# A list-scheduled attention and expert kernel: the routing chain of a chunk gets an earlier key, and row transfers by index a shorter spacing near the end

## Chip, core and metric

The kernel runs on one core of a Trainium2 chip. The metric is the device time of one execution in microseconds (us); lower is better. All arithmetic is float32.

## What is computed

The input is 16 sequences of 256 tokens with 128 channels. Four layers follow each other, each added to its input after a layer norm:

```python
x = x + attn_a(layernorm(x))   # 8 heads of 16, causal, a rank-1 term added to the scores
x = x + ffn(layernorm(x))      # 8 experts, top 2 by a router, hidden width 512
x = x + attn_b(layernorm(x))   # 16 heads of 8, no mask
x = x + ffn(layernorm(x))      # the same expert layer and weights again
```

In `ffn` each token goes to the two experts with the largest router logits; their outputs are added with softmax weights, and the sum with the token goes through one more layer norm with gamma and beta.

## The kernel before

**Layers and chunks.** The layers are called a (first attention), B (first expert layer), b (second attention) and D (second expert layer). A "batch" is one sequence of 256 tokens. The expert layers work on chunks of batches: B in chunks of 2, 4, 5 and 5 batches, D in chunks of 4, 4, 3, 2, 2 and 1. They are called B0 to B3 and D0 to D5.

**One chunk of an expert layer** (`experts`). Router logits come batch by batch (L768, kept at L777). When the last batch's logits are there, a chain of some 29 short VectorE instructions (L930 to L1100), with two groups of matmuls inside (L1005 `dt`, L1015 to L1023 `dr`), finds for each token the two rows in a list sorted by expert. Its results are `idx` (L1077, the rows), `dti` (L1100, which expert each tile of 128 rows belongs to) and, a little later, `rw` (L981, the weights). GpSimd then scatters the tokens to these rows of a DRAM buffer, 128 tokens a transfer (L1113, `xs`). SyncE loads the rows back four tiles at a time (L1158), TensorE turns them (L1169, `xt`), and for each tile multiplies by the first weight matrix (L1182, `h`), ScalarE and VectorE apply the bias and relu (L252 and L1189, `hT`), TensorE multiplies by the second (L1206, `o`), VectorE takes the result out of PSUM (L1214), and SyncE stores it (L1219, `os`). The weights of a tile's expert (578 KB) are loaded anew for each tile (L1150). GpSimd gathers the two rows of each token back, 128 tokens a transfer (L1271, `r0` and `r1`), VectorE sums them (L1296, `y`), and the last layer norm follows (L302, L304, L309 and L310 on GpSimd, L796, L804). The last chunk D5 has one batch and goes through all eight experts without sorting (L848, L861, L869, L877, L881).

**Order of the work.** Nothing is issued in the order of the source. The kernel first makes a list of tasks, each with an engine, a planned duration, what it needs, the buffers it takes, and a key. A planner at the end of the kernel walks through a clock of its own: on each engine it looks at the tasks that could start within a small slack of the earliest, and takes the one with the smallest key. Keys are counted in pairs of heads: an attention pair of heads has the key of its slot, one more for each pair; a chunk's routing chain has the key `key8`, which is the end of its last batch plus 0.2. What the planner yields is a fixed order for each engine. On the chip each engine runs its list strictly in order: an instruction that waits holds up all behind it.

**Transfers by index.** The planner also spaces these transfers: two of them start at least `GAP` = 2.6 us apart on its clock, and where ScalarE has an instruction that ends in between, the transfer is made to wait for that instruction on the chip too (`apart`), so that the spacing holds there:

```python
if t.eng == "POOL" and t.kb:
    s = max(s, moved[0] + GAP)
...
since = [i for done, i in marks if moved[0] + 1.3 <= done <= s - 0.1]
paced[0] = since[-1] if since else None
```

`all_st` holds the 192 tasks of the second kind of score matmul (L564, `st`, one for each pair of heads of both attentions), and `begun[1]` counts how many of them the planner has placed.

Of the kernel before, what the change touches and what calls it, by code (L numbers as in the profile page):

```python
# [42 lines left out]


LAT = dict(mem=3.0, qk=6.0, sh=2.4, sc=4.0, rows=4.0, we=4.5, os=5.5, g=5.0)

EARLY = 2.0

# [23 lines left out]
def block_kernel(  # L72
# [170 lines left out]
    GAP = 2.6  # L243
# [15 lines left out]
    def apart(i):  # L259
        if paced[0] is not None:  # L260
            tc.add_manual_dep(i.ins, paced[0].name, SYNC, reason="rows by index one by one")
        return i
# [99 lines left out]
    all_s, all_st = [], []  # L362

    def attention(kind, b, slot):
# [80 lines left out]
        if not (causal and b < WIDE):  # L445
# [3 lines left out]
            t_sp = Task("SP", 0.39, spread, ahead - 5, [t_sg], take=[mem_h], use=[qks_h],  # L449
                        kb=256, lat=LAT["mem"])  # L450
            if not causal and "a" in [region_of.get((i, h)) for h in halves]:
                clear = Task("DVE", 0.7, lambda: clear_k(i), ahead - 5, last + [clear])
            t_qk = [Task("SP", 1.5, spread2, ahead - 4, [t_sp, clear] + last, take=[m_h],
                         use=[mem_h], kb=256, lat=LAT["qk"])]

# [88 lines left out]
        t_ms = Task("ACT", 0.26, shift_copy, slot + pairs, [t_mt], use=[mm])  # L544
        t_sh = Task("SP", 0.56 * nq, shift2, slot + pairs, [t_ms], use=[ms_h], lat=LAT["sh"])

# [177 lines left out]
    order = {"last": None, "xs": {}, "os": {}, "n": 0}  # L724

    def experts(layer, c, ends, need, dense=False):
# [13 lines left out]
        rl_h, tgt_h, t_tgt, t_lg, tT_of = Hold("rl"), {}, {}, [], {}  # L740

        for b in bs:
            key = ends[b] + 0.2
            t0 = (b - b0) * NT

            def tgt_tile(b=b):
                g["tgt", b] = work.tile(
                    [P, NT, C], F32, tag="tgt", name=f"tgt_{n}_{b}", bufs=RINGS["tgt"]
                )
                return g["tgt", b]  # L750
            t_tgt[b], tgt_h[b] = normed(
                lambda b=b: xb[b], f"{n}_{b}", key, [at_x[b]], "tgt", tgt_tile)

            def bias(b=b):

                nc.gpsimd.tensor_tensor(
                    xb[b], xb[b], beta_sb.unsqueeze(1).to_broadcast([P, NT, C]), ALU.add
                )
            at_x[b] = Task("POOL", 0.73, bias, key + 3, [t_tgt[b]])
            t_tT, tT, tT_h = turned(  # L760
                lambda b=b: g["tgt", b], f"{n}_{b}", key, [t_tgt[b]], [tgt_h[b]])
            tT_of[b] = tT, t_tT, tT_h
            mm = Hold("mm")

            def logits(b=b, tT=tT):
                g["lg", b] = ps = ps_mm.tile([P, NT, E], F32, tag="mm", name=f"lg_{n}_{b}")
                for t in range(NT):
                    nc.tensor.matmul(  # L768
                        ps[:, t, :], lhsT=tT()[:, t * P:(t + 1) * P], rhs=wr_sb,
                        start=True, stop=True,  # L770
                    )

            def keep_logits(b=b, t0=t0):
                if b == b0:
                    g["rl"] = small.tile([P, ct, E], F32, tag="rl", name=f"rl_{n}",
                                         bufs=RINGS["rl"])
                nc.vector.tensor_tensor(  # L777
                    g["rl"][:, t0:t0 + NT, :], g["lg", b],
                    br_sb.unsqueeze(1).to_broadcast([P, NT, E]), ALU.add,
                )  # L780
            e = Task("PE", 0.26, logits, key, [t_tT], take=[mm], use=[tT_h])
            t_lg.append(Task("DVE", 0.1, keep_logits, key, [e] + t_lg[-1:], use=[mm],
                             take=[rl_h] if b == b0 else []))
# [34 lines left out]
        def every_expert(b, kk, t_gate, rw_h):  # L818
# [16 lines left out]
            def load(e):  # L835
                g["w", e] = work.tile([P, W_N], F32, tag="we", name=f"we_{n}_{e}",
                                      bufs=RINGS["we"])
                nc.sync.dma_start(out=g["w", e], in_=we[e])
# [47 lines left out]
            for e in range(E):  # L886
                w_h, hT_h, z_h, mm3 = Hold("we"), Hold("pT"), Hold("z"), Hold("mm")
                k = kk + 0.5 * e
                e_load = Task("SP", 0.5, lambda e=e: load(e), k - 8, take=[w_h],
                              kb=592, lat=LAT["we"], order=[e_load])  # L890
                t_r = []
# [12 lines left out]


        key = max(ends[b] for b in bs) + 0.2
        key8 = key
        k8 = ct * E
        per = 0.14 + 0.0011 * k8
        shape = [P, ct, E]  # L910
# [119 lines left out]
        e = Task("PE", 0.3, count, key8, chain, take=[mm1])  # L1030
        chain = [e]
        dve(0.27, total, use=[mm1])
        e = Task("PE", 0.6, ranks, key8, chain, take=[mm2])
# [77 lines left out]
        def scatter(t, k):  # L1111
            b = b0 + t // NT
            i = apart(nc.gpsimd.indirect_dma_start(  # L1113
                out=x_rows[0:ne * P, :], out_offset=bass.IndirectOffsetOnAxis(
                    ap=g["idx"][:, k, t:t + 1], axis=0),
                in_=g["tgt", b][:, t % NT, :], in_offset=None,
                bounds_check=ne * P - 1, oob_is_err=False,
            ))

            gr = f"sc_{n}"  # L1120
            tc.declare_no_dep(i.ins, group=gr, reason="each row is written once")
            tc.add_to_no_dep_group(gr, i.ins)
        t_sc = []
        free = order["xs"].get(q, []) + zeroed[q]
        for k in range(2):
            for t in range(ct):
                b = b0 + t // NT
                t_sc.append(Task(
                    "POOL", 1.25, lambda t=t, k=k: scatter(t, k), key + 0.3 + 0.01 * len(t_sc),
                    [t_idx[k]] + free, use=[idx_h, tgt_h[b]], kb=64, lat=LAT["sc"] - 1.3,  # L1130
                ))

# [92 lines left out]
        for i in range(ne):  # L1225
            b, j = divmod(i, TB)
            kk = tile_key(i)
            w_h, hT_h, mm1, mm2 = Hold("we"), Hold("hT"), Hold("mm"), Hold("mm")
            if j == 0:
                x4_h, xT_h, mm3, o4_h = Hold("x4"), Hold("xT"), Hold("mm"), Hold("o4")  # L1230
                e = Task("SP", 0.4, lambda b=b: rows(b), kk - 2.5, t_sc, take=[x4_h],
                         kb=256, lat=LAT["rows"])
                t_rows.append(e)
                e = Task("PE", 0.46, lambda b=b: turn_rows(b), kk - 1, [e],
                         take=[mm3, xT_h], use=[x4_h])
                t_xT = Task("ACT", 0.48, lambda b=b: keep_rows(b), kk - 1, [e], use=[mm3])
                t_out = []
            t_load = Task("SP", 0.95 if j == 0 else 0.5, lambda i=i: load(i), kk - 3,
                          [t_ti], take=[w_h], use=[ti_h], kb=592, lat=LAT["we"], order=[t_load])
            t_up_last = t_up = Task("PE", 0.98, lambda i=i: up(i), kk, [t_load, t_xT],  # L1240
                                    take=[mm1, hT_h], use=[w_h, xT_h], order=[t_up_last],
                                    kind="up")
            t_up.rate = RATES[layer][min(c, len(RATES[layer]) - 1)]
            r1 = Task("DVE", 0.27, lambda i=i: relu_v(i), kk, [t_up], use=[mm1, w_h])
            r2 = Task("ACT", 0.76, lambda i=i: relu_s(i), kk, [t_up], use=[mm1, w_h])
            t_dn = Task("PE", 0.98, lambda i=i: down(i), kk, [r1, r2],
                        take=[mm2, o4_h] if j == 0 else [mm2], use=[hT_h, w_h],
                        order=t_dns[-1:])
            t_dns.append(t_dn)
            t_out.append(Task("DVE", 0.2, lambda i=i: keep_out(i), kk, [t_dn], use=[mm2, w_h]))  # L1250
            loads.append(t_load)
            if j == TB - 1 or i == ne - 1:
                stores.append((i, Task(
                    "SP", 0.4, lambda b=b: store(b), kk, t_out + order["os"].get(q, []),
                    use=[o4_h], kb=256, lat=LAT["os"], lag=LAG_OS)))
# [22 lines left out]
        for b in bs:  # L1278
# [3 lines left out]
            for k in range(2):  # L1282
                r_h = Hold(f"r{k}")
                e = [None]
# [52 lines left out]
    ends = {"B": {}, "D": {}}  # L1337
# [16 lines left out]
    begun = [0.0, 0]  # L1354
    moved = [-GAP]
# [11 lines left out]
    def start(t):  # L1367
        s = max(t.ready + t.lag, free[t.eng])
        if t.eng == "POOL" and t.kb:
            s = max(s, moved[0] + GAP)  # L1370
        if t.kind == "up" and len(all_st) > begun[1]:
            s = max(s, begun[0] + t.rate)
        for h in t.take:
            q, n = rings[h.ring], RINGS[h.ring]
            if len(q) >= n:
                if q[-n].left:
                    return None
                s = max(s, q[-n].done)
            if h.ring == "att" and len(q) > 1:
                if q[-1].left or q[-2].left:  # L1380
                    return None
                s = max(s, q[-1].done, q[-2].done)
        return s
# [34 lines left out]
    while left:  # L1418
        best = None
        for e in ENGS:  # L1420
# [4 lines left out]
            s, t = min(((s, t) for s, t in c if s <= s0), key=lambda st: st[1].key - stay(st[1]))  # L1425
# [3 lines left out]
        s, t, c = best  # L1429
# [94 lines left out]
```

## Time and profile before

| | |
|---|---|
| median of three runs | 945.51 us (942.85 to 948.49) |
| the profiled execution: time, span | 950.31 us, 948.6 us |
| TensorE busy | 889.4 us, 94% of the span |
| VectorE, ScalarE, GpSimd busy | 618.1, 512.6 and 416.9 us |
| indexed transfers, GpSimd time for one | 248, about 1.0 us |
| bytes moved by DMA | 181.96 MB, mean 192 GB/s |
| mean granted TensorE clock | 0.978 |

The profiled execution took 1.7 us more than its span from the first to the last instruction, and 4.8 us more than the median. Every matmul of the source appears twice in the trace. In the rows of the profile PE is TensorE, DVE VectorE, ACT ScalarE, POOL GpSimd and SP SyncE; a name behind "<-" in brackets says what ended a wait.

### The profile page before, as it was taken

The numbers are of one execution on the slowest core, as the hardware profiler recorded it, in microseconds if no ns is written. First come the engines' busy times: TensorE is split into PE (matmuls) and PEld (weight loads), VectorE is DVE, ScalarE is ACT, GpSimd is POOL, SyncE is SP. The second block draws the span as 40 slices with busy tenths as digits, with TensorE's granted clock in tenths as the row PEclk, the third lists the DMA queues.
The fourth block names the chain that finished last, engine by engine and source line by source line (L and its number), as shares of the span: only waits on it lengthen the run. The fifth ranks groups of instructions, "written<-read, shape, count | busy, mean of one in ns | idle before, by whom it ended". The sixth has DMA issues, their size and how long they took to land. (4 is left out here: it accounts for less than half of the span.)

```text
span 948.6 us, 24346 instructions
## 1 busy us (share of the span) xinstructions
PE 889.4 (94%) x8941; PEld 720.4 (76%) x8941; DVE 618.1 (65%) x1919; ACT 512.6 (54%) x1188; POOL 416.9 (44%) x553
## 2 busy tenths in 40 slices
PE   7788899998999999999999999999989999899995
PEld 5555688887887778787777777777767877799985
DVE  4578687778657757456686457745766665564666
ACT  5355565665555664565655555556645655545421
POOL 4134635654653554313554225443534314444633
PEclk9799899999999999999999999999999999999998
DMA  4222667666765587575776767566856675599991
GB/s 128 57 70 73 232 194 208 202 208 194 232 187 186 165 207 183 187 204 176 186 197 192 221 180 202 168 190 208 188 142 192 216 185 166 170 306 348 372 316 36
DMA packets 115191, 181.96 MB, mean 192 GB/s; under 512 B 11904, under 2 KB 79360, under 8 KB 115072
## 3 DMA queue, kind: packets, MB, share of 16 engines
q1 hardware_dynamic: 106704, 163.69, 58.4%
q0 software_dynamic: 7936, 16.27, 5.5%
q8 instruction: 71, 1.16, 0.5%
q10 hardware_dynamic: 432, 0.45, 0.2%
q14 instruction: 48, 0.39, 0.1%
HBM read 145.63 MB, written 34.34 MB: 190 GB/s over the span
## 5 line engine op out<-in xcount | busy, mean ns | idle before, releaser
L510 DVE TENSOR_REDUCE m_b<-s_b 128x4 f32<-128x1024 f32 x128 | 155.8, 1220 | 59.9 <-PE s_b L487 39.5
L252 ACT ACTIVATE pT_b<-st_b 128x1024 f32<-128x1024 f32 x128 | 129.9, 1026 | 68.4 <-PE st_b L564 49.2
L252 ACT ACTIVATE hT_D<-h_D,we_D 128x128 f32<-128x128 f32 (+1 forms) x301 | 89.7, 372 | 103.2 <-issue 34.5
L487 PE MATMUL s_b<-qk 31*128 31x256 f32 x1024 | 134.9, 405 | 4.7 <-DVE m_b L510 3.1
L564 PE MATMUL st_b<-qk 32*128 32x256 f32 x1024 | 131.4, 409 | 3.7 <-issue 1.7
L252 ACT ACTIVATE hT_B<-h_B,we_B 128x128 f32<-128x128 f32 x276 | 81.1, 365 | 75.0 <-DVE hT_B L1189 38.6
L1206 PEld LDWEIGHTS o_D<-we_D,hT_D 128*128 128x128 f32 x760 | 93.6, 192 | 23.6 <-ACT hT_D L252 12.0
L1206 PE MATMUL o_D<-we_D,hT_D 128*128 128x128 f32 x760 | 107.1, 287 | 4.5 <-ACT hT_D L252 2.6
L1206 PE MATMUL o_B<-we_B,hT_B 128*128 128x128 f32 x736 | 106.3, 288 | 3.4 <-ACT hT_B L252 2.8
L1206 PEld LDWEIGHTS o_B<-we_B,hT_B 128*128 128x128 f32 x736 | 90.7, 192 | 24.4 <-ACT hT_B L252 14.2
L1182 PE MATMUL h_D<-xT_D,we_D 128*128 128x128 f32 x760 | 102.4, 282 | 0.1
L1271 POOL DMA_INDIRECT r_B<-os,idx_B x64 | 67.9, 1062 | 75.7 <-DMA we_B<-in_we_dram 21.0
L1182 PE MATMUL h_B<-xT_B,we_B 128*128 128x128 f32 x736 | 100.6, 280 | 0.2 <-ACT xT_B L252 0.2
L1182 PEld LDWEIGHTS h_D<-xT_D,we_D 128*128 128x128 f32 x760 | 92.5, 193 | 9.9 <-issue 7.4
L1113 POOL DMA_INDIRECT xs<-tgt_D,idx_D x60 | 60.1, 1001 | 87.7 <-DVE idx_D L1077 17.9
L1182 PEld LDWEIGHTS h_B<-xT_B,we_B 128*128 128x128 f32 x736 | 89.7, 192 | 10.3 <-issue 8.6
L487 PEld LDWEIGHTS s_b<-qk 31*128 31x128 f32 x1024 | 80.8, 186 | 17.7 <-issue 5.5
L564 PEld LDWEIGHTS st_b<-qk 32*128 32x128 f32 x1024 | 79.1, 188 | 17.2 <-issue 7.2
L1271 POOL DMA_INDIRECT r_D<-os,idx_D x60 | 62.8, 1047 | 62.0 <-ACT hT_D L252 30.4
L1113 POOL DMA_INDIRECT xs<-tgt_B,idx_B x64 | 64.7, 1011 | 50.7 <-ACT hT_B L252 12.8
L500 DVE TENSOR_TENSOR s_a<-s_a,cmask 128x512 f32<-128x512 f32 x64 | 44.6, 697 | 42.7 <-PE s_a L487 22.5
L1189 DVE TENSOR_SCALAR hT_D<-h_D,we_D 128x128 f32<-128x128 f32 x95 | 33.0, 350 | 56.7 <-PE h_D L1182 23.7
(401 smaller groups left out, 1620.0 us busy)
## 6 DMA issues: line engine op xcount, KB each, us to landing
we_D<-in_we_dram SPq DMA_DIRECT2D x103, 578.0 KB
we_B<-in_we_dram SPq DMA_DIRECT2D x92, 578.0 KB
qk<-qkm SPq DMA_DIRECT2D x104, 64.0 KB
x_B<-xs SPq DMA_DIRECT2D x20, 256.0 KB
os<-o_B SPq DMA_DIRECT2D x20, 256.0 KB
x_D<-xs SPq DMA_DIRECT2D x20, 256.0 KB
os<-o_D SPq DMA_DIRECT2D x20, 256.0 KB
qkm<-qks_b SPq DMA_DIRECT2D x16, 256.0 KB
```

Source lines behind the costliest of these rows:

```text
L252: i = getattr(nc.scalar, name)(*args, **kw)
L487: nc.tensor.matmul(ps[:, j, col:col + nk], lhsT=qT[r:r + 31, t * P:(t + 1) * P], rhs=kT[r:r + 31, 0:nk], start=True, stop=True,)
L500: nc.vector.tensor_tensor(dg, dg, cmask.unsqueeze(1).unsqueeze(1).to_broadcast([P, 2, 2, P]), ALU.add,)
L510: nc.vector.tensor_reduce(m[:, :, heads].rearrange("p t j -> p j t"), ps.rearrange("p j (t k) -> p j t k", k=T), axis=AX.X, op=ALU.max, ne ...
L564: nc.tensor.matmul(ps[:, j, col:col + T - q0], lhsT=kT[r:r + 32, t * P:(t + 1) * P], rhs=qT[r:r + 32, q0:T], start=True, stop=True,)
L1113: i = apart(nc.gpsimd.indirect_dma_start(out=x_rows[0:ne * P, :], out_offset=bass.IndirectOffsetOnAxis(ap=g["idx"][:, k, t:t + 1], axis=0) ...
L1182: nc.tensor.matmul(ps[:, f, :], lhsT=w[:, f * P:(f + 1) * P], rhs=g["xT", b][:, j * P:(j + 1) * P], start=True, stop=True,)
L1189: nc.vector.tensor_scalar(g["hT", i][:, f, :], g["h", i][:, f, :], g["w", i][:, W_B1 + f:W_B1 + f + 1], 0.0, ALU.add, ALU.max)
L1206: nc.tensor.matmul(ps, lhsT=g["hT", i][:, f, :], rhs=g["w", i][:, W_2 + f * C:W_2 + (f + 1) * C], start=(f == 0), stop=(f == NF - 1),)
L1271: apart(nc.gpsimd.indirect_dma_start(out=g["r", k, b][:, t, :], out_offset=None, in_=o_rows[0:ne * P, :], in_offset=bass.IndirectOffsetOnAxis(
```

## The change

It has three live parts (the first and the third number of `AHEAD` are zero and alter nothing):

```diff
+AHEAD = 0, 6, 0
...
-        key8 = key
+        key8 = key - AHEAD[1]
...
                 e = Task("PE", 0.46, lambda b=b: turn_rows(b), kk - 1, [e],
-                         take=[mm3, xT_h], use=[x4_h])
+                         take=[mm3, xT_h], use=[x4_h], order=[order.get("turn")])
+                order["turn"] = e
...
         if t.eng == "POOL" and t.kb:
-            s = max(s, moved[0] + GAP)
+            s = max(s, moved[0] + (GAP if len(all_st) > begun[1] + 24 else 1.4))
```

- The tasks of the routing chain up to `dti` get a key that is smaller by six pairs of heads. The four tasks of the weights `rw` keep theirs (`gates` sets `key8` anew).
- The turns of rows (`turn_rows`, L1169) are placed in the order of the chunks and blocks; before, a later block could be turned first.
- Once at most 24 of the 192 `st` tasks are left to place, the spacing of transfers by index drops from 2.6 to 1.4 on the planner's clock.

No instruction is added or taken away on any engine. The order changes on all of them.

More of the change, by code (lines that the diff above doesn't have):

```diff
@@ L742, in experts @@
         for b in bs:
-            key = ends[b] + 0.2
+            key = ends[b] + 0.2 - AHEAD[0]
             t0 = (b - b0) * NT
@@ L1128, in experts @@
                 t_sc.append(Task(
-                    "POOL", 1.25, lambda t=t, k=k: scatter(t, k), key + 0.3 + 0.01 * len(t_sc),
+                    "POOL", 1.25, lambda t=t, k=k: scatter(t, k), key + 0.3 - AHEAD[2] + 0.01 * len(t_sc),
                     [t_idx[k]] + free, use=[idx_h, tgt_h[b]], kb=64, lat=LAT["sc"] - 1.3,
```

## The prediction

> **What bounds the kernel now.** I read the page first (engines, then the slices), then windows, then the waits of each engine, then timelines around the stalls.
>
> ```profile
> span 948.6 us, 24346 instructions
> PE 889.4 (94%) x8941; PEld 720.4 (76%) x8941; DVE 618.1 (65%) x1919; ACT 512.6 (54%) x1188; POOL 416.9 (44%) x553
> PE   7788899998999999999999999999989999899995
> DMA  4222667666765587575776767566856675599991
> ```
>
> PE is at work for 94% of the span, and no other engine comes near. The whole prize is 948.6 - 889.4 = 59 us of idle PE. The windows say where it lies:
>
> ```profile
> 0.00:25.00 25.00, 17.89 (x106) 14.02 (x106) 12.35 (x48) 14.65 (x33) 10.48 (x29) 1.00 0.44 121
> 650.00:700.00 50.00, 46.52 (x488) 36.29 (x488) 32.45 (x98) 29.82 (x62) 21.52 (x29) 0.97 0.73 188
> 875.00:900.00 25.00, 24.90 (x211) 24.03 (x210) 15.25 (x61) 13.07 (x44) 15.26 (x18) 1.00 1.02 373
> 925.00:949.00 24.00, 13.97 (x96) 12.98 (x94) 15.73 (x55) 3.35 (x8) 9.10 (x12) 0.89 0.12 34
> ```
>
> The columns are PE, PEld, DVE, ACT, POOL, clock, DMA. The first four windows (0 to 100) leave 20.5 us of PE idle. There the PE list of the changed program is the same as before (its first difference is at PE instruction 637 of 4774, about 100 us in). 100 to 600 leaves 15 us, 600 to 825 leaves 12, the rest 12, of which 10 are the last drain. From 850 on the DMA engines are full (1.02) and PE is too.
>
> What a stall looks like, in the timeline of DVE at 689 and of POOL before it:
>
> ```profile
> 683.59 1.12 POOL L1271 DMA_INDIRECT r_D<-os,idx_D  x1 [0.19 <-ACT hT_D L252]
> ...
> 691.63 0.35 DVE L1296 SCALAR_TENSOR_TENSOR y_D<-r_D,rw_D,tgt_D 128x128 f32<-128x128 f32 x1 [2.26 <-DMA r_D<-os,idx_D]
> 692.01 1.22 DVE L510 TENSOR_REDUCE m_b<-s_b 128x4 f32<-128x1024 f32 x1
> ```
>
> DVE reached a sum `y` whose gathered rows had not landed, and stood 2.26 us; behind it in its list was the maximum `m_b`, for which PE waited 2.52 us. The same at the end, milder:
>
> ```profile
> 900.66 6.34 DMA r_D<-os,idx_D
> 907.09 0.35 DVE y_D L1296
> 907.44 0.21 DVE o_D L1214
> 907.65 0.14 issue
> 907.79 1.29 PE o_D L1206 x8
> ```
>
> This is the chain of waits: gather, `y`, the eviction `o_D` behind it, PE, which lost 1.0 us.
>
> Whether the routing chain is late anywhere: for D4, the tightest of the later chunks, the timelines show its last `idx`, the last scatter, the load of its first rows, the turn of these rows.
>
> ```profile
> 843.67 0.16 DVE L1077 CAST idx_D<-dsf_D 128x4 int32<-128x4 f32 x1
> 859.94 0.99 POOL L1113 DMA_INDIRECT xs<-tgt_D,idx_D  x1 [1.24 <-ACT xT_D L252]
> 865.46 0.38 SPq L1158 DMA_DIRECT2D x_D<-xs  x1
> 873.07 0.60 PE L1169 MATMUL xt_D<-ident,x_D 128*128 128x128 f32 x4
> ```
>
> 29 us pass between the places and their first use. For D0 it is 70 (471.44 to 541.13). PE works on other tiles meanwhile. No stall of PE in the trace ends on a row load. So the chain is on no path.
>
> **Part 1, the earlier key.** Nothing is added, so what counts is the order of the two built programs. The chain cannot begin before the last logits, and each step needs the one before, so a smaller key only wins ties against `m_b`, `hT` and evictions. In DVE's list the last `idx` moves by a place or two up to B2 and comes later in D: place 1233 to 1249 for D1, 1674 to 1691 for D4. So "sooner" is hardly delivered, and with 29 us of cover it is worth 0. It may cost: one step is 0.16 to 0.28 us, 29 of them for each of nine chunks, all in front of something PE needs would be some 50 us; none would be 0. To choose I compared the two PE lists. Each full 128-column pass costs 0.112 us (L869, x32 in 3.57 us in the chain). For each task that needs ACT or DVE work on an earlier PE result I took the PE work in between, and counted what it lacks to the lag at which such tasks stall in the trace (1.4 us for `o` after `h`, 0.85 to 2.2 for others). The lacks sum to 71 us before and 73 after; 1.4 of the difference is one place at the very end, costed below. Attention pairs stand two by two in both, and PE changes between its kinds of work 458 times before, 454 after. So part 1 is costed at 0, with 5 either way: that much lies between stretches of the two lists (150 to 200: 4.6 against 2.3; 300 to 350: 2.3 against 4.4). Its cover is PE work of other tiles; without it D4 would show first.
>
> **Part 2, turns in order.** Before, `xt` of D3's first block stands ahead of D2's last; now behind it. 0.33 us of PE work changes places with 0.44. 0.
>
> **Part 3, the closer spacing.** It begins with the pairs of batch 13 (743 us) and touches 60 transfers: D3's and D4's scatters, D1's to D4's gathers. Of these 39 waited for an ACT instruction before, 10 now. Such waits hold the rows of D up by
>
> ```profile
> POOL r_D L1271 <- ACT hT_D L252: 30.4, 19, 3.5
> ```
>
> (total, times, longest). Freed, POOL issues every 1.30 us (0.99 of work, 0.30 of issue). What this buys, place by place:
>
> - D4's scatters: 17.6 us from first to last before, 9.1 now. But the places come later: `dr` of D4 moves from 717.5 to 721.1 us of PE work, its first turn from 751.1 to 750.0, so cover falls from 33.6 to 28.9. Needed: 5 (ranks to `idx`) + 9.1 + 5.5 (last scatter to row load, 859.94 to 865.46) + at most 7.6 (load to turn) = 27.2. It fits, with 1.7 to spare: 0.
> - D3's gathers: 891.8 to 909.6 before; now eight in 10 us. The stall at 907 goes: -1.0.
> - The end. Before, batch 14 ends last since its gathers are issued until 938.66; x15 is done at 942.48, x14 at 945.39. Now the sums of batches 13 and 14 come earlier and x15 ends last: of the 2.9 between the two about 2.1 goes, since 0.6 to 0.8 of batch 14's work still stands ahead of x15. But the PE list now ends o5, o6, h7, o7 where it ended h6, h7, o6, o7. o7 needs `hT` of expert 7, and DVE has before that four `y` (1.2), z and two sums (1.05), statistics (0.75), and `hT` itself (0.88) behind o6's end at about 935.5 and the rest of z5: o7 starts at 938.9 in place of 937.2, +1.7. With DVE's tail behind it the last instruction comes at about 945.5 against 945.39: 0.
> - POOL's queue: batch 14's and 15's norm steps and `bias` stand among gathers in both lists. In SP's list 163 of 811 instructions stand elsewhere among the rest, and the weights' loads keep their order among themselves. The chip shows SP waiting for free buffers most of the time, which PE sets: 0.
>
> Sum: -1.0. The profiled execution goes from 950.3 to 949.3; it was 4.8 above the median, so I put the median at 945.5 - 1.0 = 944.5.
>
> **Two rules against rows.** The gather at 683.59 held DVE until 691.63, 8.0 us; the one in the chain took 6.34. The Trainium skill (DMA: Bandwidth & Descriptors, Anatomy of one DMA) has 2.0 us + bytes / 436e3 for a GpSimd transfer, 2.15 for 64 KB (an estimate by that page). By the rule no gather is ever late here, neither stall exists and closer spacing gains nothing: 945.5. By the rows it can remove stalls of 1.0 and 2.5, or add them. I go by the rows.
> PE's clock in the window around the first stall:
>
> ```profile
> 686.00:698.00 12.00, 9.48 (x99) 6.94 (x94) 7.40 (x26) 4.29 (x9) 3.59 (x4) 0.86 0.68 151
> ```
>
> 0.86 over 12 us is 3.4 us at half clock, 1.7 lost, after 2.5 us of idling. TensorE: Matmul & The Clock Gate (Part 1) lets the clock fall after an idle window of about 3.4 us. By the page a stall of 2.5 costs 2.5, by the row 4.2. I price a long stall at 4.2; two are then 8.4, not 5.0.
>
> **Rivals.** *Slower: sums stand too early in DVE's list.* The planner now believes the rows come 1.4 apart and puts D1's and D2's sums directly among `hT` and `o_D` of D2 and D3, tile by tile; y of D0's batch 1 also moves ahead by a tile, and its second gather comes behind one more transfer. DVE is strictly in order. From the point at which a gather lands more than about 1.2 us after DVE reaches its sum (the lead PE has over an `hT`), PE stops; past 2 us the clock falls too. Two such hits: 945.5 - 1.0 + 8.4 = 953. For it: the 6 to 8 us above, DMA at 1.02 in just this stage. Against it: only 7.1 us, five waits, were lost so before, and most of D1's gathers now come ahead of the full stage.
>
> *Faster: the long stalls go.* 693 (4.2), 714 (1.7 idle, also followed by half clock: 3.4) and 907 (1.0) vanish: 945.5 - 8.6 = 937. For it: 30.4 us of waits on ACT leave POOL. Against: only 907 lies behind 743, where the spacing changes; at 714 PE waits for a shift whose cover in the new list is 4.8 us of PE work against 5.2, so it should return.
>
> *It doesn't do what it says.* For the chain I take this as the main case.
>
> **Numbers.** A difference of 0.5%, 4.7 us, is about what a measurement of this kernel can tell from no change. Main case, within it: 0.44, 941 to 950. Slower by over 0.5%: 0.32; a reordering of all lists has more ways to meet a late row than to lose one. Faster: 0.24. The range 937 to 957 takes in both rivals, the 5 us of part 1, and a third hit.
>
> **What would show it.** Right: POOL's waits on ACT in the last 200 us far fewer, gathers 1.3 apart, no PE gap at 907, PE's last matmul about 1.7 later with x15 last, PE busy within 1 us of 889. Slower: new DVE waits `y_D <- DMA r_D` between 790 and 910 with PE gaps and clock dips behind them. Wrong: a stretch from 100 to 740 us that changes by more than 5 us, or a PE wait on `xt` of D4.

## The result, and the profile after

In the first comparison the changed kernel took 982.6 us (979.43 to 986.52, 4 runs) and the kernel before 946.43 us (942.85 to 948.49, 4 runs): a ratio of 1.0388, 95% interval 1.0338 to 1.0438. That is slower, by 36 us, and far outside the forecast range of 937 to 957. On one of the chips of the experiments below, the same kernel took 935.47 us beside 930.0 (ratio 1.0061, interval 1.0038 to 1.0083). The two belong to different chips: beside the one the kernel before took 946.43 us, beside the other 930.0. The experiments ran on five.

The profiled execution behind the traces of this section ran 979.43 us. First the page of the changed kernel, the lines that answer to those shown of before:

```profile
span 977.7 us, 24333 instructions
PE 894.6 (91%) x8941; PEld 722.0 (74%) x8941; DVE 615.0 (63%) x1919; ACT 513.6 (53%) x1188; POOL 415.9 (43%) x553
PE   7788899999899999999999999999999789948996
...
PEclk9799999999899999999999999999999989979998
DMA  4122866766686767676766756576677446849881
```

The same work runs on every engine; the 13 instructions fewer are waits. A slice is 24.4 us. PE's row holds its nines, but for one 8, until 758 us, then has a 7 and an 8, and a 4 from 855 to 880; the DMA row has a 4 at all three places, where before it stood at 9 from 830 us on. The windows say how much, the changed kernel first, the kernel before second (columns PE, PEld, DVE, ACT, POOL, clock, DMA share, GB/s):

```profile
100.00:740.00 640.00, 617.61 (x6546) 496.28 (x6547) 430.50 (x1280) 369.15 (x838) 296.49 (x380) 0.99 0.68 196
760.00:800.00 40.00, 32.95 (x310) 24.84 (x303) 18.43 (x51) 16.32 (x34) 16.79 (x18) 0.87 0.44 134
850.00:900.00 50.00, 35.21 (x293) 32.87 (x292) 15.76 (x67) 15.99 (x52) 21.90 (x23) 0.86 0.72 237
```

```profile
100.00:740.00 640.00, 616.14 (x6449) 494.76 (x6445) 427.70 (x1263) 363.80 (x828) 294.06 (x378) 0.99 0.68 194
760.00:800.00 40.00, 39.20 (x434) 30.76 (x434) 26.16 (x73) 22.10 (x45) 11.76 (x13) 1.00 0.67 184
850.00:900.00 50.00, 49.37 (x419) 47.81 (x418) 28.75 (x121) 24.95 (x82) 28.47 (x33) 1.00 1.01 360
```

From 100 to 740 us PE idles 1.5 us less than before. From 760 to 800 it idles 7.1 instead of 0.8, from 850 to 900 14.8 instead of 0.6. Between the two traces the span grew by 29.1: idle time of PE by 23.9 (977.7 - 894.6 against 948.6 - 889.4), 20.4 of it in these two windows, and busy time by 5.2, on an unchanged number of matmuls, because the clock fell (0.87 and 0.86 in these windows).

What happens there is seen best in the timeline of PE in the changed kernel from 853 us, when GpSimd issues sixteen transfers by index, D4's eight scatters and eight gathers of D2, one every 1.30 us from 853.05 to 873.69 (start, duration, what; in brackets the idle time before it and what ended it):

```profile
854.14 1.16 PE L1184 MATMUL h_D<-xT_D,we_D 128*128 128x128 f32 x8
855.14 1.95 PE L1208 MATMUL o_D<-we_D,hT_D 128*128 128x128 f32 x16
858.47 1.39 PE L1208 MATMUL o_D<-we_D,hT_D 128*128 128x128 f32 x8 [1.38 <-issue]
859.70 1.06 PE L1184 MATMUL h_D<-xT_D,we_D 128*128 128x128 f32 x8
861.98 1.16 PE L1184 MATMUL h_D<-xT_D,we_D 128*128 128x128 f32 x8 [1.22 <-issue]
866.26 2.08 PE L1184 MATMUL h_D<-xT_D,we_D 128*128 128x128 f32 x8 [3.12 <-issue]
876.66 1.65 PE L1208 MATMUL o_D<-we_D,hT_D 128*128 128x128 f32 x6 [8.32 <-ACT hT_D L254]
```

The last three `h` tiles end at 860.8, 863.1 and 868.3. DVE does its half of the matching `hT` only from 875.8 on, all three in a row (timeline of DVE):

```profile
869.50 0.29 DVE L1216 TENSOR_TENSOR o_D<-o_D,we_D 128x128 f32<-128x128 f32 x1 [3.30 <-PE h_D L1184]
875.80 0.87 DVE L1191 TENSOR_SCALAR hT_D<-h_D,we_D 128x128 f32<-128x128 f32 x3 [6.01 <-remote]
```

So DVE stood 6 us although by PE's rows the first of these results had long been finished. Nothing in DVE's own list stood in the way, and no row of a transfer was late: from 743 us on the trace has no wait of DVE on `r_D` and none of PE on `xt_D`. PE's signal that it was done came late; and PE itself paused three times (1.38, 1.22, 3.12) with "issue", that is, with no releaser that the profile shows. All of it ended two microseconds after GpSimd's last transfer. The trace also records when a semaphore (the counter by which one engine tells another that a result is ready) is raised, and this says the same without any consumer. Each recorded signal was set beside the last instruction that had ended by then and that gives such a signal. In this trace TensorE's come up to 7.6 us behind that end; those of DVE, ACT and GpSimd 0.01 (median), and never more than 0.03 in any trace. Where transfers by index fill over 60% of the 3 us before, TensorE's are 0.50 late on average; elsewhere 0.06. This lateness of signals is what is called late completions below. The last 15 us of a run are left out of it: there every trace, whatever its kernel or chip, has TensorE signals 9 us or more behind. One limit of the measure: the end of a matmul in the trace is modelled, so a late completion can be a signal that came late or a matmul that really ended late, and the trace can't tell the two apart.

The same sign was in the trace of before, small, and the prediction passed over it. Timelines of before around 805 us, of PE:

```profile
803.68 1.93 PE L613 MATMUL av_b<-pT_b,v 128*32 128x256 f32 x32
...
809.30 0.44 PE L699 MATMUL ot_b<-ident,avs_b 128*128 128x128 f32 x2 [2.38 <-ACT avs_b L252]
```

of ACT:

```profile
808.66 0.59 ACT L252 COPY avs_b<-av_b 128x512 f32<-128x512 f32 x1 [3.55 <-remote]
```

and of POOL:

```profile
804.15 1.12 POOL L1271 DMA_INDIRECT r_D<-os,idx_D  x1 [1.05 <-ACT pT_b L252]
805.58 1.00 POOL L1271 DMA_INDIRECT r_D<-os,idx_D  x1 [0.30 <-issue]
806.88 0.99 POOL L1271 DMA_INDIRECT r_D<-os,idx_D  x1 [0.30 <-issue]
```

`av` ends at 805.61, ACT takes it at 808.66, 3.05 us later, with three gathers back to back in between. Signals of TensorE are up to 2.1 us late here, the most in this trace. It is no fixed toll of three transfers, though: before has eight runs of three or four that start less than 1.6 us apart, and this is the one that costs PE over 2 us. Beside the other seven it idles 0 to 1.4 (0.66 at the three scatters from 507.16 to 509.70).

### The profile page after: what moved, and what is told of

Its sections match the earlier page's. It is cut to its first block, busy times and chain, and to the rows that moved or that the text cites. A ratio compares the mean times of both kernels' runs of the same rounds, so it can differ in the third digit from the quotient of the medians.

```text
span 977.7 us, 24333 instructions
## 1 busy us (share of the span) xinstructions
PE 894.6 (91%) x8941; PEld 722.0 (74%) x8941; DVE 615.0 (63%) x1919; ACT 513.6 (53%) x1188; POOL 415.9 (43%) x553
## 5 line engine op out<-in xcount | busy, mean ns | idle before, releaser
L489 PE MATMUL s_b<-qk 31*128 31x256 f32 x1024 | 140.5, 405 | 3.4 <-ACT pT_b L254 2.1
L566 PE MATMUL st_b<-qk 32*128 32x256 f32 x1024 | 137.3, 405 | 2.3 <-DVE m_b L512 1.8
L1208 PE MATMUL o_D<-we_D,hT_D 128*128 128x128 f32 x760 | 109.1, 290 | 19.6 <-ACT hT_D L254 16.9
L254 ACT ACTIVATE hT_B<-h_B,we_B 128x128 f32<-128x128 f32 x276 | 81.8, 368 | 85.7 <-DVE hT_B L1191 29.1
L1184 PE MATMUL h_D<-xT_D,we_D 128*128 128x128 f32 x760 | 105.4, 284 | 4.6 <-issue 4.3
L489 PEld LDWEIGHTS s_b<-qk 31*128 31x128 f32 x1024 | 83.4, 186 | 16.0 <-ACT pT_b L254 5.3
L566 PEld LDWEIGHTS st_b<-qk 32*128 32x128 f32 x1024 | 82.4, 186 | 16.1 <-issue 4.8
```

The source lines that it names most:

```text
L254: i = getattr(nc.scalar, name)(*args, **kw)
L489: nc.tensor.matmul(ps[:, j, col:col + nk], lhsT=qT[r:r + 31, t * P:(t + 1) * P], rhs=kT[r:r + 31, 0:nk], start=True, stop=True,)
L566: nc.tensor.matmul(ps[:, j, col:col + T - q0], lhsT=kT[r:r + 32, t * P:(t + 1) * P], rhs=qT[r:r + 32, q0:T], start=True, stop=True,)
L1184: nc.tensor.matmul(ps[:, f, :], lhsT=w[:, f * P:(f + 1) * P], rhs=g["xT", b][:, j * P:(j + 1) * P], start=True, stop=True,)
L1208: nc.tensor.matmul(ps, lhsT=g["hT", i][:, f, :], rhs=g["w", i][:, W_2 + f * C:W_2 + (f + 1) * C], start=(f == 0), stop=(f == NF - 1),)
```

## The experiments

Five chips were used; kernels that are compared below with one ratio ran on the same chip as their kernel before. By the time of the kernel before they fall into two kinds: 949.1 and 950.3 us on two of them, 929.9, 930.0 and 930.1 on three, called calm below. (Each was used in one sitting only, so "chip" here can also mean a state that the chip was in.)

**Is it the spacing?** `e1` keeps the earlier key and the ordered turns but spaces by 2.6 us to the end; `e2` is the kernel before with only the closer spacing. Both on a chip with 949.1 us for the kernel before.

```
e1, from after:
-            s = max(s, moved[0] + (GAP if len(all_st) > begun[1] + 24 else 1.4))
+            s = max(s, moved[0] + GAP)
e2, from before:
-            s = max(s, moved[0] + GAP)
+            s = max(s, moved[0] + (GAP if len(all_st) > begun[1] + 24 else 1.4))
```

> The changed kernel with the spacing of indexed transfers back at 2.6 to the end; earlier chain key and ordered turns stay. Theory 1 (back-to-back indexed transfers on GpSimd hold up TensorE's completions): 940 to 952, no TensorE gap over 3 us, no completion later than 2.5 us behind the end that the trace shows. Theory 2 (the new order of the lists, above all the last attention batch and D4's chain pushed behind D2's tiles, makes the stalls): 970 to 985.

> The kernel before with the 1.4 spacing alone, no earlier key, no ordered turns. Theory 1: 965 to 990, with completions 3 to 8 us late inside runs of transfers at 1.3 us. Theory 2: 940 to 955.

Measured: e1 948.61 us, ratio 0.9964 (0.9925 to 1.0002); e2 991.03, ratio 1.0398 (1.0305 to 1.0491). The spacing alone makes a loss like that of the whole change (1.0388 in the first comparison; the changed kernel itself did not run on this chip); the other two parts make none here.

**Is it the order of the lists that the spacing brings, or the transfers being close?** `e4` is the kernel before with every engine's list unchanged and only the waits of GpSimd's transfers on ScalarE taken out, so that GpSimd issues as soon as data and buffers allow. `e3` is the changed kernel, its lists unchanged, with a memset of 1.2 us behind each of the 61 last transfers. Same chip.

```
e4, from before, in apart():
-        if paced[0] is not None:
+        if False:
e3, from after, behind each late transfer:
+            if t.eng == "POOL" and t.kb and len(all_st) <= begun[1] + 24:
+                nc.gpsimd.memset(idle, 0.0)      # 128x1344
```

> The kernel before, every list the same, but no indexed transfer waits for a ScalarE instruction any more, in the whole kernel. Theory 1: bursts wherever several transfers stand together in GpSimd's list, late completions in all stages, 960 to 1000. Theory 2: 940 to 950, the waits only delay rows that nobody needs yet.

> The changed kernel, every list the same, but after each of the 61 late indexed transfers GpSimd fills a scratch tile (128x1344, about 1.25 us), so that they start some 2.6 us apart again. Theory 1: the 20 us lost between 850 and 880 come back, late completions go, 945 to 960 (rows come later by the fill, which may cost a few us). Theory 2: 975 to 995, since the order is the same and GpSimd is slower.

Measured: e4 1020.3 us, ratio 1.0719 (1.0631 to 1.0806). With no list changed, letting the transfers run costs nearly twice what the change cost; late completions (over 1 us) appear all along the run from 300 us on, up to 12.8 us. e3 missed: 997.47, ratio 1.049 (1.041 to 1.057). Its trace has no completion later than 0.9 us, and from 740 us on, where the memsets stand, none later than 0.28, against 7.6 in the changed kernel: in that respect the expectation held, but the time went elsewhere. The waits of PE in e3 (total, times, longest):

```profile
PE tp_D L352 <- ACT tgt_D L255: 26.7, 2, 19.2
PE o_D L1209 <- ACT hT_D L255: 18.4, 9, 7.5
```

`tgt_D` needs GpSimd's `lnr_D`, which stood behind a row of padded transfers, until 904.11:

```profile
902.92 1.23 POOL L1445 MEMSET idle<- 128x1344 f32 x1
904.11 0.24 POOL L312 TENSOR_SCALAR lnr_D<-mv_D 128x2 f32<-128x2 f32 x1
```

The longest wait on `hT_D`, 7.5, has the same root. ACT's and DVE's work there stands behind a sum `x` that waited for GpSimd; the window around it shows GpSimd busy for 23.23 of 25 us:

```profile
818.29 0.61 DVE L807 SCALAR_TENSOR_TENSOR x<-y_D,lnr_D_4y,x 128x128 f32<-128x128 f32 x2 [5.59 <-POOL lnr_D_4y L313]
800.00:825.00 25.00, 17.52 (x176) 14.28 (x175) 9.87 (x34) 7.00 (x16) 23.23 (x23) 0.86 0.45 130
```

The filler swapped one loss for another: GpSimd, at 2.4 us per transfer, became the bound of the tail. As a remedy it is useless; as a test it shows that transfers 2.4 us apart no longer hold PE's signals up, and that a GpSimd busy for over nine tenths of the time does not do so by itself, on a chip with the hold-up.

**The suspect by itself.** Twelve extra gathers of 64 KB, into a tile nobody reads, were put into the kernel before at a place where GpSimd has nothing else to do for 20 us and PE idles 0.04 of 30 us; beside it twelve memsets of 1.0 us, the twelve gathers 2.4 us apart, and twelve plain transfers. The lines that set up `probe`, `pidx` and `idle` are left out.

```
e5, from before, behind the bias add of x2:
+                if n == "D0" and b == 2:
+                    for j in range(12):
+                        nc.gpsimd.indirect_dma_start(
+                            out=probe[:, j, :], out_offset=None, in_=x[0:NBE * T, :],
+                            in_offset=bass.IndirectOffsetOnAxis(ap=pidx[:, 0:1], axis=0),
+                            bounds_check=NBE * T - 1, oob_is_err=False,
+                        )
e6, in its place:
+                        nc.gpsimd.memset(idle[:, 0:1060], 0.0)
e7, behind each gather of e5:
+                        nc.gpsimd.memset(idle, 0.0)
e8, in its place:
+                        nc.gpsimd.dma_start(out=probe[:, j, :], in_=x[j * P:(j + 1) * P, :])
```

> The kernel before, with 12 extra gathers by index (64 KB each, rows of the input into a tile that nobody reads), one right behind another, after the bias add of x2 that GpSimd does at 413.6 us. In the kernel before GpSimd has nothing but that add between 412 and 435 us, and TensorE idles 0.04 of the 30 us from 400 to 430. The outputs are as before. Theory 1 (back-to-back transfers by index hold up TensorE's completions): from some 416 to 430 us evictions start several us after the matmuls whose results they read, TensorE gets idle stretches of 5 to 15 us in all, and the whole run gets 5 to 15 us longer, 954 to 964 beside 949. Theory 2 (the order of the lists made the loss, transfers close together cost nothing): no new idle time, within 2 us of before.

> The kernel before, with 12 memsets of 128x1060 (near 1 us each) in GpSimd's list at the place where the other kernel of this call has its 12 gathers. Theory 1: GpSimd being busy isn't what holds TensorE up; no new idle time on TensorE, within 2 us of before. If it were GpSimd's occupation as such[...], idle time like that of the 12 gathers would show, 5 us or more.

> The kernel before, with the same 12 gathers at the same place, but a memset of 128x1344 (1.2 us) behind each, so one gather every 2.4 us instead of every 1.3. Same number and bytes of transfers. Theory 1, as a matter of density: no completion late by over 1 us, no new idle time, within 2 us of before. If each transfer held TensorE up by its own share however far apart they are, the loss would be that of the 12 back-to-back gathers.

> The kernel before, with 12 plain transfers of 64 KB (no index; rows of the input into the same unread tile) issued by GpSimd one behind another at the same place. Tells whether the index matters. If it is what GpSimd does for a transfer of 128 rows, whatever says where they lie, that holds TensorE up: idle time and loss like that of the 12 gathers by index, 5 to 15 us. If it is the index: no new idle time, within 2 us of before. I expect the first a little more than the second.

Measured, beside 929.89 us: e5 933.64, ratio 1.0036 (1.0011 to 1.0061); e6 930.47, 1.0003 (0.9983 to 1.0024); e7 936.68, 1.0068 (1.0046 to 1.0091); e8 934.35, 1.0035 (1.0010 to 1.0061). The first theory failed here: PE was as full during the twelve gathers as ever (the second of the two window lines below). But so did the sign in the kernel before: on this chip no completion was later than 0.31 us in any of the four traces (those over 0.10 all at 84 us), and the kernel before was 19 us faster than on the chip of e1 to e4. e7 missed as well: the spaced gathers, expected within 2 us, cost 6.8, more than the burst. Of this 2.5 lie between 430 and 460 us, behind the memsets, where PE is busy for 26.48 us against 29.02 in e6; where the rest lies is open. All this gave a third theory: the hold-up belongs to some chips, or to a state that a chip stays in.

**The same kernels on other chips.**

> The changed kernel, once more. On the chip of the four probes no completion of TensorE was late by over 0.1 us in any of them, not even in the paced bursts of the kernel before, whose median there was 929.9 us beside 949.1 on the chip of the first four experiments: so the hold-up may belong to the chip, or to a state of it, and not to every chip. Theory 3 (the hold-up of completions comes on some chips only): where the kernel before runs near 930 us and no completion is late, the changed kernel is within 10 us of it on either side; where it runs near 946 or more, the changed kernel is 3 to 5% slower. Theory 1 as first put (back-to-back transfers hold TensorE up everywhere, and the twelve gathers of the probe were only not the kind): 3 to 5% slower on any chip.

> The kernel before without the waits of GpSimd's transfers on ScalarE (every engine's list the same), once more. Theory 3: 6 to 8% slower where the kernel before takes 946 us or more, within 2% where it takes near 930 us. Theory 1 as first put: 6 to 8% slower on any chip.

> The kernel before with the 12 extra gathers back to back behind the bias add of x2, once more. Theory 3: where the kernel before takes 946 us or more, TensorE's completions come late in these 16 us and the loss is 5 to 15 us; where it takes near 930 us, no late completion and within 0.5%. If the twelve gathers are harmless also where the changed kernel loses 3 to 5%, then transfers close together aren't enough, and something of the last stages has to come with them.

These came to a chip with 950.32 us for the kernel before. Measured: e9, the changed kernel, 986.45 us, ratio 1.0342 (1.0297 to 1.0386); e10 1014.16, ratio 1.0690 (1.0648 to 1.0733); e11, the twelve gathers, 969.65, ratio 1.0231 (1.0174 to 1.0289). The third theory hit on the first two. On the third it hit in kind and not in size: the gathers cost 19.3 us where it allowed 5 to 15. Completions are up to 6.3 us late in e9 and 4.5 in e11. The windows of the twelve gathers, on this chip (e11) and on that of e5:

```profile
413.00:428.00 15.00, 10.42 (x79) 7.25 (x74) 3.27 (x5) 3.48 (x8) 11.65 (x12) 0.71 0.73 175
```

```profile
405.00:420.00 15.00, 14.96 (x172) 11.42 (x168) 7.64 (x11) 9.35 (x20) 11.65 (x12) 1.00 0.95 238
```

One program, one stage, the same 11.65 us of GpSimd: 79 matmuls get through on the one chip and 172 on the other, and with PE stop the engines that it feeds (DVE 3.3 against 7.6, ACT 3.5 against 9.4).

Not all of the 19.3 us is lost there. Matmul by matmul against the trace of before, e11 loses 10.9 us between 415 and 433 and 5.0 more between 516 and 531. The second place is a run of three scatters of the kernel's own, with late completions of 2.0 beside it:

```profile
515.08 0.97 POOL L1126 DMA_INDIRECT xs<-tgt_D,idx_D  x1 [2.21 <-ACT qks_b L258]
516.36 0.97 POOL L1126 DMA_INDIRECT xs<-tgt_D,idx_D  x1 [0.30 <-issue]
517.63 0.98 POOL L1126 DMA_INDIRECT xs<-tgt_D,idx_D  x1 [0.30 <-issue]
520.32 1.39 PE L1219 MATMUL o_B<-we_B,hT_B 128*128 128x128 f32 x8 [2.40 <-ACT hT_B L258]
```

Beside the same three scatters PE idles 0.66 us in before. So the twelve gathers themselves cost about 11.

The two kinds of chip differ in one more thing that the traces show. On those with the hold-up, and in the first comparison, 5 to 17% of the semaphore signals of TensorE, VectorE and ScalarE are missing from the trace (before: 1576 of 1745, 1545 of 1808 and 1008 of 1140 are there); on the calm ones under 1%. The gaps spread over the run, not over the bursts alone. So the taking of the trace is a rival that stays open: every timed execution on record comes with a span and a granted clock, and none shows whether an execution without a trace is held up too.

> The kernel before with 12 memsets of 1.0 us at the place of the 12 gathers, once more. On the chip of the first probes it cost nothing (1.0003), but nor did much the gathers there; on another, where the kernel before takes 950 us, the 12 gathers cost 19 us. Theory 3: where the kernel before takes 946 us or more, still nothing, within 0.5%: it is transfers that hold TensorE up, not a busy GpSimd. If a busy GpSimd did it: 10 to 20 us.

> The kernel before with the 12 gathers 2.4 us apart (a memset behind each), once more. Theory 3 with density as the trigger: where the kernel before takes 946 us or more, no completion late by over 1 us in these 29 us; what is left is what the chip of the first probes showed, 7 us (GpSimd's own later work late, TensorE waiting 1.9 us for tgt_D at 438), so 5 to 9 us. If each transfer holds TensorE up however far apart: 20 us or more.

> The kernel before with 12 plain transfers of 64 KB from GpSimd back to back (0.53 us each on the chip of the first probes), once more. If the index is what counts: within 1% where the kernel before takes 946 us or more. If any transfer that GpSimd itself spells out row by row counts: completions late and 5 to 19 us. I expect the second a little more than the first.

> The changed kernel a third time, on whatever chip this call gets. Theory 3: where the kernel before takes near 930 us, within 10 us of it on either side (the forecast's step, that freed transfers cost nothing and buy a few us, would hold there); where it takes 946 us or more, 3 to 5% slower again.

These came to a chip with 930.0 us for the kernel before. e12 1.0017 (0.9995 to 1.0040); e13 1.0111 (1.0056 to 1.0166); e14 1.0050 (1.0024 to 1.0077). On a calm chip they repeat e6 to e8 (e13 costs 10.6 us, over the 5 to 9 expected) and can't tell what these kernels do on a chip with the hold-up. e15 tells more: the changed kernel takes 935.47 us, ratio 1.0061 (1.0038 to 1.0083). Its own run of sixteen transfers, 832.3 to 853.0:

```profile
832.00:852.00 20.00, 20.00 (x194) 19.23 (x187) 9.58 (x37) 10.29 (x34) 15.09 (x16) 1.00 0.96 313
```

and the changed kernel of the first comparison, over the sixteen transfers shown above:

```profile
853.00:873.00 20.00, 9.61 (x80) 7.98 (x72) 2.65 (x12) 2.09 (x7) 15.37 (x16) 0.83 0.60 181
```

PE 20.00 of 20 us against 9.61. The stall of before at 809 is gone too. On this calm chip, in the kernel before with the memsets (e12) the same task has the same three gathers beside it (786.28, 787.70, 789.00). Its timelines, of PE and of ACT:

```profile
785.81 1.93 PE L619 MATMUL av_b<-pT_b,v 128*32 128x256 f32 x32
```

```profile
787.81 0.59 ACT L258 COPY avs_b<-av_b 128x512 f32<-128x512 f32 x1 [0.57 <-PE av_b L619]
```

`av` ends at 787.74 and ACT starts 0.07 us later, where it was 3.05.

**What the other parts cost, and whether wider spacing helps.** `e16` is e8 once more, `e17` is e1 again, and `e18` is e1 with

```
-    GAP = 2.6
+    GAP = 3.2
```

> The kernel before with 12 plain transfers of 64 KB from GpSimd back to back, a third time; the first two chips showed no hold-up in anything, and it cost 0.35 and 0.5%. If this chip holds TensorE's completions up (the kernel before at 946 us or more): late completions and 10 to 20 us, if any transfer that GpSimd spells out row by row counts; within 1% if it is the index.

> The changed kernel with the spacing of 2.6 us kept to the end (the earlier places and the ordered turns alone), once more, for a tighter interval than the 0.9925 to 1.0002 of the first. By the forecast's steps (both parts on no path): within 0.3% on either side on any chip.

> The same, with 3.2 us between transfers instead of 2.6 everywhere (GAP, which the planner of the lists uses): a version that might beat both. If the short bursts that are left in the kernel before cost it something on a chip with the hold-up: 2 to 6 us faster there. If rows then come late for their users: 2 to 10 us slower, on any chip, with TensorE waiting for transfers in the last 200 us.

They came to a third calm chip, 930.06 us for the kernel before. e16 1.0108 (1.0057 to 1.0158), again with no late completion, so it settles nothing on plain transfers. e17 934.22 us, ratio 1.0049 (1.0028 to 1.0070), a little outside what was expected: on this chip the earlier key and the ordered turns cost 4 to 5 us. The windows of e17 and of e12, whose lists are those of before but for the memsets:

```profile
100.00:600.00 500.00, 485.96 (x5236) 394.62 (x5230) 348.59 (x1042) 292.44 (x678) 237.38 (x311) 1.00 0.71 204
```

```profile
100.00:600.00 500.00, 490.37 (x5241) 398.58 (x5234) 350.11 (x1041) 295.01 (x678) 249.08 (x322) 1.00 0.70 203
```

4.4 us of PE idling more, in small waits; the longest of them, 1.8 us, is PE waiting for `hT_D`. Between e15 (1.0061, on another calm chip) and e17 (1.0049) no difference can be told: without the hold-up the closer spacing shows neither gain nor loss. e18 956.88, ratio 1.0316 (1.0275 to 1.0357): 26.8 us, far beyond the 2 to 10 that were expected of the bad case, and no better version. With 3.2 us between transfers PE is busy for 476.39 of the 500 us from 100 to 600, 9.6 less than in e17, in many small waits. None of the kernels run beats the kernel before beyond its interval.

## Why the prediction was wrong

- *Part 1, the earlier key, costed at 0 with 5 either way, and part 2, at 0.* Together 0.9964 on a chip with the hold-up, an interval that touches 1, and 1.0049 on a calm one, 4.6 us: within the stated 5. Why the two differ wasn't tried, so which of them holds for the chip of the first comparison is open. The stretch from 100 to 740 us changed by 1.5 us, less than the 5 named as a refutation, and PE waits for no `xt` of D4: the chain is on no path, as said.
- *Part 3: "Freed, POOL issues every 1.30 us."* It does; the waits of its gathers on ACT's `hT_D` in the last 220 us fell from 15 to 5 (in time only from 23.5 to 22.1 us, since one of the five took 14.4), D4's scatters went out in 9.1 us. The waits of DVE on gathered rows, 4.9 us in four before, are gone, and x15 ends last. So the step's mechanics held.
- *The step that failed is what it charged for this: nothing.* "It fits, with 1.7 to spare: 0" and "now eight in 10 us" counted only what the transfers need and deliver. What a run of them does to PE was no term of the sum, nor of any rival. By e1 and e2 it is the loss of the first comparison, 36 us; between the two traces 29.1, 23.9 of idle PE and 5.2 of busy time beside the lower clock. On a calm chip the charge of nothing stands, as far as e15 and e17 can tell; the prediction knew nothing of two kinds of chip, and being right there would have been luck. By which path the transfers hold TensorE up stays open.
- *The slower rival* had the right sign and the wrong cause. It wanted late rows, waits `y_D <- DMA r_D` between 790 and 910; there are none. Its price of 8.4 for two hits was also too small: in the single hold-up from 853 to 878 us PE is busy for 10.95 us of 25.
- *The rows against the rule on the cost of one transfer* (the fit in the Trainium skill, DMA: Bandwidth & Descriptors, Anatomy of one DMA) turned out beside the point: no loss comes from when rows land.
- *The rule on the clock* (the Trainium skill, TensorE: Matmul & The Clock Gate, Part 1: the clock falls after an idle window of about 3.4 us). The trace of before had half clock after 2.5 us of idling; here it follows again at 866.26, where eight matmuls take 2.08 us behind 3.12 of idling instead of the 1.06 of 859.70. So the rows decide, and pricing a stall above its length was right in kind. Its size was too large for these stalls: the busy time grew by 5.2 us beside 23.9 of new idling, about 0.2 for each, where the prediction's row had 1.7 for 2.5. The stated sign "PE busy within 1 us of 889" failed by this growth (894.6).
- *What would have warned.* The stall at 809, 2.38 us, larger than the 1.0 at 907 on which the gain was built, was on no list of the prediction. Its rows put ACT 3.05 us behind a finished `av` with three transfers at 1.3 us beside it. Reading that row to its end would have given a rival with a price: here 3 transfers held PE for 2.4 us, the change makes runs of 16. A rival and no more, since the other short runs in before cost PE little.

## What to carry to other kernels

A wait that looks like pure loss on an engine that isn't the bound can be protecting the bound. Before taking pacing out, look for a place in the old trace where it happened to be missing, and read what the busiest engine did there (one quiet place is not enough: the short runs in this trace differed); a consumer that starts microseconds after its producer's last row, with nothing of its own in the way, is the sign. And try a timing change on more than one chip before giving it a sign: this one is 3.4 to 3.9% slower on some and 0.6% on another.

## What the runs showed of the hardware

- On two chips, and in the first comparison, GpSimd's transfers by index, 64 KB each and 1.3 us apart, hold TensorE: its signals come up to 12.8 us behind the end that the trace gives for the matmul (e4), and it pauses itself without a releaser in the trace. Twelve of them at a quiet place made the run 19.3 us longer (969.65 against 950.32), about 11 of it at that place. A run of three can show it (2.4 us at 805 in before) and need not (0.66 at 507). Completions of VectorE, ScalarE and GpSimd weren't late by over 0.03 us in any trace.
- On three other chips none of it shows: no signal of TensorE later than 0.31 us in eleven traces, and the kernel before is 2% faster (930 us against 949 and 950).
- Spaced 2.4 us apart by memsets on a chip with the hold-up (e3), the transfers made no completion late by over 0.28 us.
- Open: what the two kinds of chips differ in, and whether it is the chip or a state of it; whether the hold-up comes without a trace being taken; by which path the transfers reach TensorE; whether plain transfers from GpSimd do the same (e8, e14 and e16 all ran on calm chips, at a cost of 0.35 to 1.1%).
